# Side work of a graph-attention kernel in finer steps, and a PSUM row handed on by halves

## The chip, the cores and the metric

The kernel runs on one core of one Trainium2 chip. The metric is the device time of one execution in microseconds; the kernel before took 1645.74 us (median of three, 1645.39 to 1646.08). The core has five engines with queues of their own: TensorE (PE, matmul and transposes; PEld is its weight load), VectorE (DVE), ScalarE (ACT), GpSimd (POOL) and SyncE (SP, which issues transfers). Each works through its own instructions in order and waits where an operand or a buffer is not ready.

## The reference

Eight graphs (B = 8) of N = 2048 nodes with F = 64 features share one adjacency matrix `adj`. Four layers follow each other, each with a residual and a normalisation over the features. Layers 0 to 2 are graph attention; cut to what matters:

```python
h = x @ W                                   # layer 0 also scales x by node, and normalises h
s1, s2 = h @ a1, h @ a2                     # one score per node each
e = leaky_relu(s1[:, :, None] + s2[:, None, :], 0.2)
att = softmax(where(adj > 0, e, -big), axis=-1)
out = elu(att @ h)                          # layer 0: att @ h + h; layer 2: relu
x = layernorm(x + out)
# layer 3: softmax over neighbours of softplus features, per feature, then the same residual
```

A row without any neighbour gets the mean of `h`.

## The kernel before

A **unit** is one layer of one graph, with K = 16 steps, one for each block of 128 source nodes. There are 24 units in this order: layers 0 and 1 for graphs 0 to 3 (units 0 to 7), the same for graphs 4 to 7 (units 8 to 15), then layer 2 for all eight (units 16 to 23). Layer 3 runs beside layer 2 and after it.

In layers 0 and 1 the exponential of the leaky score is taken apart: up to a factor that softmax cancels it is `exp(s2[j]) * max(exp(0.8 s1[i]), exp(-0.8 s2[j]))`. So the kernel keeps a row `r` of exp(0.8 s1) for all 2048 nodes, spread over 128 partitions in PSUM, and one step is one VectorE instruction on 128x2048 and eight matmul records (four products of 512 columns, each in two fp32 passes):

```python
def spread(layer, b):                       # the row of the next unit, from three bf16 pieces
    sc = S[layer, b]
    sc.r = Banks.pool.tile([P, N], F32, tag="b", name=f"r_{layer}_{b}")   # one buffer of four banks
    for c in range(NCH):                    # NCH = 4
        sl = slice(c * 512, (c + 1) * 512)
        pe.matmul(sc.r[:, sl], lhsT=ones3, rhs=sc.r3[:, sl], start=True, stop=True)

def attend(u, jb, last):                    # one step; layer 2 cut
    w = work.tile([P, N], F32, tag="w", name=f"w_{u.n}_{jb}", bufs=4)
    dve.scalar_tensor_tensor(w, s.r, s.e[:, 1, jb : jb + 1], edge[:, jb, :], ALU.max, ALU.mult)
    if jb == K - 1:
        last()                              # hands over: spread() of the next unit
    for c in range(NCH):
        pe.matmul(sums[c], lhsT=s.v[:, jb, :], rhs=w[:, c * 512 : (c + 1) * 512],
                  start=(jb == 0), stop=False)
    # after the last step: the three-row product of mean and emptyT closes the sums
```

In layer 2 the step is a clamp on GpSimd, two exponentials on ScalarE into PSUM and two products of 128x1024 on VectorE.

Everything else is **side work**, written as generators. `bg.step()` is called once per step of a unit and lets each running generator go on to its next `yield`; `yield 2` lets one call pass. So a `yield` decides behind which step's instructions the rest is queued on each engine.

```python
def finish(u):                              # after a unit; cut
    for c in range(2):
        act.copy(oT[:, c], u.acc[c])        # out of PSUM
    ...
    while done < 4:
        width = Banks.width()               # PSUM tiles to use at once: 2, or 1 in layer 2
        ...                                 # per tile: two matmuls, p_o <- oT, RH
        yield 2 if pairs and width == 2 else 1      # pairs: layer 3 has begun
        ...                                 # den = 1 / p_o (DVE), o = p_o * den (ACT)
    ...                                     # residual and elu on ACT and POOL, with yields
    pool.tensor_tensor(o, o, e, ALU.add)
    e_slots.give()
    yield 1
    nm, rs = yield from stats(o, K, f"x_{u.n}")     # sums on DVE, st_x; power -1/2 on POOL
    yield 1
    for k in range(K):                      # xn <- o, normalised, 16 small ACT instructions
        ...
        if k % K2 == K2 - 1:                # K2 = 8
            yield 1

def scores(layer, b):                       # s1, s2 of the next layer of the graph; cut
    yield from transposed(xT, sums, V[layer, b].v, f"{n}v")
    p = psum(f"p_s_{n}")
    for q in range(K2):
        pe.matmul(p[:, 4 * q : 4 * q + 4], lhsT=xT[:, q], rhs=AS[layer], start=True, stop=True)
    for h in range(2):                      # the mean over the nodes, from two partial sums
        pe.matmul(p[:, 64 : 64 + F], lhsT=sums[:, h : h + 1].to_broadcast([P, P]),
                  rhs=ident2, start=(h == 0), stop=(h == 1))
    ...                                     # exponentials, row to memory, mean

def features0(b):                           # h, scores and row of layer 0; cut
    for k in range(K):
        act.activation(xs[:, k], x[:, k], AF.Identity, scale=..., bias=...)
        if k == K2 - 1:
            yield 1
    yield 1
    ...                                     # transposes, products p_h, squares, st_h
    ...                                     # row to memory (row_d)
    for k in range(K2): ...                 # y <- h, eight ACT instructions
    yield 1
    for k in range(K2, K): ...
    ...                                     # sums for the mean on POOL, p_mean
```

`prepare` fetches the next unit's row (`row`) and forms `pv` = V * exp(s2) on GpSimd once the row is there, from step 10 of the unit before; where it is not there in time the loop runs side work until it is. After units 7 and 15, `group` prepares layer 2 for four graphs at once; its core is a log-sum-exp `p_lse` of 256 small matmuls over the adjacency blocks, two row blocks at a time for the first group. Main loop, cut:

```python
for n, (layer, b) in enumerate(todo):
    now[0] = layer
    for jb in range(K):
        attend(u, jb, handover)
        if jb == K - 1:
            ...                             # finish(u), then scores(layer + 1, b), then group
        elif not done and jb >= 10 and ready(*nxt):
            prepare(*nxt); done = True
        if layer == 0 and jb == 4 and 2 <= b + 2 < B:
            bg.add(features0(b + 2))        # graphs 0 and 1: before and at unit 0
        bg.step()
    while not done:
        bg.step() ...
    handover()
```

Of the kernel before, what the change touches and what calls it, by code (L numbers as in the profile page):

```python
# [8 lines left out]
F32 = mybir.dt.float32  # L9
# [5 lines left out]
ALU = mybir.AluOpType  # L15
AX = mybir.AxisListType

P = 128
# [30 lines left out]
def gnn4_kernel(ctx: ExitStack, tc: tile.TileContext, t, out):  # L49
# [438 lines left out]
    def stats(y, n, name):  # L488

        st = small.tile([P, 2, n], F32, tag="st", name=f"st_{name}", bufs=4)  # L490
        yield from sq_slots.take()
        sq = tmp.tile([P, n, F], F32, tag="sq", name=f"sq_{name}")
        act.activation(sq, y, AF.Square)
        dve.tensor_reduce(st[:, 0], y, AX.X, ALU.add)
        yield 1
        dve.tensor_reduce(st[:, 1], sq, AX.X, ALU.add)
        sq_slots.give()
        yield from inv_std(st, n, name)
        return st[:, 0], st[:, 1]
# [88 lines left out]
    def features0(b):  # L588

        n = f"0_{b}"  # L590
        x = x_cur[b].v
        xs = early.tile([P, K, F], F32, tag="xs", name=f"xs_{b}", bufs=1)
        for k in range(K):
            act.activation(
                xs[:, k],
                x[:, k],
                AF.Identity,
                scale=nodes[:, k : k + 1],
                bias=nodes[:, K + k : K + k + 1],
            )  # L600
            if k == K2 - 1:
                yield 1
        yield 1
        yield from xT_slots.take()
        xT = tmp.tile([P, K2, P], F32, tag="xT", name=f"xT_{b}")
        sums = small.tile([P, 2], F32, tag="sums", name=f"sums_{b}", bufs=4)
        yield from transposed(xT, sums, xs, n)
        yield from h_slots.take()
        h = tmp.tile([P, K, F2], F32, tag="h", name=f"h_{b}")
        g0 = 0  # L610
        while g0 < 4:
            width = Banks.width()
            ps = []
            yield from pm_slots.take(width)
            for g in range(g0, min(g0 + width, 4)):
                p = psum(f"p_h_{b}_{g}")
                for k in range(2):
                    pe.matmul(
                        p[:, k * 2 * F2 : (k + 1) * 2 * F2],
                        lhsT=xT[:, 2 * g + k],  # L620
                        rhs=w0c.rearrange("p h f -> p (h f)"),
                        start=True,
                        stop=True,
                    )
                ps.append((g, p))
            yield 1
            for g, p in ps:
                act.copy(
                    h[:, 4 * g : 4 * g + 4, :], p[:, : 4 * F2].rearrange("p (k f) -> p k f", f=F2)
                )  # L630
            pm_slots.give(width)
            g0 += width
        xT_slots.give()
        yield from sq_slots.take()
        sq = tmp.tile([P, K, F], F32, tag="sq", name=f"sq_h_{b}")
        act.activation(sq, h[:, :, :F], AF.Square)
        yield 2
        st = small.tile([P, 2, K], F32, tag="st", name=f"st_h_{b}", bufs=4)
        dve.tensor_reduce(st[:, 1], sq, AX.X, ALU.add)
        sq_slots.give()  # L640
        yield from inv_std(st, K, f"h_{b}", centered=True)
        rs = st[:, 1]
        sc = S[0, b] = Scores()
        s = small.tile([P, 2, K], F32, tag="s0", name=f"s_{n}")
        dve.tensor_tensor(
            s, h[:, :, F:].rearrange("p k w -> p w k"), bc_k(rs, 2, K), ALU.mult
        )
        dve.tensor_tensor(s, s, bc_f(s_off, 2, K), ALU.add)
        exponentials(sc, s[:, 0], s[:, 1], s, 0, b, n)()

        yield from pm_slots.take()
        p = psum(f"p_r_{n}")
        pe.transpose(p[:K, :P], sc.e[:, 0], ident)
        yield 1
        rows_term(sc, p[:K, :P], n, 0, b)
        pm_slots.give()
        y = rows_tile(early, "y", f"y_{b}")
        for k in range(K2):
            act.activation(y.block(k), h[:, k, :F], AF.Copy, scale=rs[:, k : k + 1])
        yield 1  # L660
        for k in range(K2, K):
            act.activation(y.block(k), h[:, k, :F], AF.Copy, scale=rs[:, k : k + 1])
        y.settle()
        V[0, b] = y
        src = y.v
        for m in (8, 4, 2, 1):
            pool.tensor_tensor(h[:, :m, :F], src[:, :m], src[:, m : 2 * m], ALU.add)
            src = h[:, :, :F]
        yield 4
        yield from pm_slots.take()  # L670
        p = psum(f"p_mean_{n}")
        pe.matmul(p[:, :F], lhsT=ones, rhs=h[:, 0, :F], start=True, stop=True)
        h_slots.give()
        yield 1
        yield from mean_pieces(sc, p[:, :F], n)

    def scores(layer, b):

        n = f"{layer}_{b}"
        sc = S[layer, b] = Scores()  # L680
        yield from xT_slots.take()
        xT = tmp.tile([P, K2, P], F32, tag="xT", name=f"xTv_{n}")
        sums = small.tile([P, 2], F32, tag="sums", name=f"sumsv_{n}", bufs=4)
        yield from transposed(xT, sums, V[layer, b].v, f"{n}v")
        yield from pm_slots.take()
        p = psum(f"p_s_{n}")
        for q in range(K2):
            pe.matmul(
                p[:, 4 * q : 4 * q + 4], lhsT=xT[:, q], rhs=AS[layer], start=True, stop=True
            )  # L690
        s = p[:, : 4 * K2].rearrange("p (q r w) -> p w q r", r=2, w=2)
        for h in range(2):
            pe.matmul(
                p[:, 64 : 64 + F],
                lhsT=sums[:, h : h + 1].to_broadcast([P, P]),
                rhs=ident2,
                start=(h == 0),
                stop=(h == 1),
            )
        xT_slots.give()  # L700
        yield 1 if b == B - 1 else 2
        if layer == 2:
            g = groups2[b // NB]
            if b % NB == 0:
                g.s = small.tile([P, 2, NB, K], F32, tag="s", name=f"s_{n}", bufs=1)
            act.copy(g.s[:, :, b % NB].rearrange("p w (q r) -> p w q r", r=2), s)
            bg.add(mean_pieces(sc, p[:, 64 : 64 + F], n), begun=True)
        else:
            s1 = small.tile([P, 2, K], F32, tag="s0", name=f"s_{n}")
            act.copy(s1.rearrange("p w (q r) -> p w q r", r=2), s)  # L710
            top = exponentials(sc, s1[:, 0], s1[:, 1], s1, layer, b, n)
            bg.add(mean_pieces(sc, p[:, 64 : 64 + F], n), begun=True)
            yield from pm_slots.take()
            p = psum(f"p_r_{n}")
            pe.transpose(p[:K, :P], sc.e[:, 0], ident)
            yield 1
            top()
            rows_term(sc, p[:K, :P], n, layer, b)
            pm_slots.give()
# [24 lines left out]
    def spread(layer, b):  # L744

        sc = S[layer, b]
        sc.r = Banks.pool.tile([P, N], F32, tag="b", name=f"r_{layer}_{b}")
        for c in range(NCH):
            sl = slice(c * 512, (c + 1) * 512)
            pe.matmul(sc.r[:, sl], lhsT=ones3, rhs=sc.r3[:, sl], start=True, stop=True)  # L750
# [6 lines left out]
    def group(gi):  # L757
# [61 lines left out]
        yield 1  # L819

        am = small.tile([P, NB, K], F32, tag="am", name=f"am_{nm}", bufs=1)
        slots = pl_slots if Banks.shared else pm_slots
        yield from slots.take()
        Banks.busy += 1
# [74 lines left out]
    def attend(u, jb, last):  # L899

        s = u.s
        if u.layer < 2:
            w = work.tile([P, N], F32, tag="w", name=f"w_{u.n}_{jb}", bufs=4)
            dve.scalar_tensor_tensor(
                w, s.r, s.e[:, 1, jb : jb + 1], edge[:, jb, :], ALU.max, ALU.mult
            )
        else:
            w = ahead[u.b, jb]
            if jb + 2 < K:
# [27 lines left out]
    def finish(u):  # L937
# [16 lines left out]
        while done < 4:  # L954
# [16 lines left out]
            done += width  # L971
            if done >= 4:
                oT_slots.give()
            yield 2 if pairs and width == 2 else 1
            for c, s0, p in ps:
                p4 = p[:, : 4 * F1].rearrange("p (s h f) -> p s h f", s=2, h=2)
                den = small.tile([P, 2, 2], F32, tag="den", name=f"den_{u.n}_{c}_{s0}")
# [22 lines left out]
        else:  # L1000
# [15 lines left out]
            yield 1  # L1016
            pool.tensor_tensor(o, o, e, ALU.add)
            e_slots.give()
            yield 1
        nm, rs = yield from stats(o, K, f"x_{u.n}")  # L1020
        xn = Rows(x_cur[b].t, layer < 2)
        if layer == 2:
# [3 lines left out]
        else:  # L1026
            yield 1
            for k in range(K):
                act.activation(
                    xn.block(k), o[:, k], AF.Identity, scale=rs[:, k : k + 1], bias=nm[:, k : k + 1]  # L1030
                )
                if k % K2 == K2 - 1:
                    yield 1
            xn.settle()
        o_slots.give()
# [7 lines left out]

    pairs = []

    now = [0]

    def l3_features(b):

# [199 lines left out]
    def flags():  # L1249
# [12 lines left out]
        dve.tensor_tensor(beyond[0:1, :], beyond[0:1, :], top[0:1, 1:2], ALU.max)  # L1262
        dve.tensor_scalar(flag, beyond[0:1, :], 0.0, None, ALU.is_gt)

    for n, (layer, b) in enumerate(todo):
        if (layer, b) == (2, 1):
            early_.close()
# [2 lines left out]
        if (layer, b) == (2, 5):  # L1270
            bg.add(flags())
        u = unit(layer, b)
        now[0] = layer
        nxt = todo[n + 1] if n + 1 < len(todo) else None
        done = nxt is None

# [6 lines left out]
        def handover():  # L1283
# [3 lines left out]
            if in_psum(*nxt):  # L1287
                if n == 0:
                    Banks.use("psR", 1)
                spread(*nxt)  # L1290
            elif nxt == (2, 0):
                Banks.use("psE", 2)
# [4 lines left out]
        for jb in range(K):  # L1297
# [22 lines left out]
                load_x(b + 4)  # L1320
            if n == 0 and jb == 3:
                bg.add(constants())
            if layer == 0 and jb == 4 and 2 <= b + 2 < B:
                bg.add(features0(b + 2))
            bg.step()
        while not done:
            bg.step()
# [515 lines left out]
```

## Time and profile before

| | busy us | share of the span of 1643.8 us |
|---|---|---|
| PE, matmuls | 1349.0 | 82% |
| PE, weight loads (beside matmuls) | 667.2 | 41% |
| DVE | 1301.1 | 79% |
| ACT | 802.8 | 49% |
| POOL | 823.7 | 50% |

The parts of the run, cut where the closing matmuls of units 0, 15 and 23 end:

| part | from, to (us) | PE busy | DVE busy | POOL busy |
|---|---|---|---|---|
| start and unit 0 | 0 to 105.7 | 61.0 | 71.8 | 26.4 |
| units 1 to 15, layers 0 and 1 | 105.7 to 839.2 | 622.4 | 631.1 | 254.8 |
| units 16 to 23, layer 2 beside layer 3 | 839.2 to 1396.5 | 469.9 | 465.8 | 435.2 |
| rest of layer 3 | 1396.5 to 1643.8 | 195.7 | 132.5 | 107.3 |

How to read the lines that follow in the prediction. Instructions are named by engine, operation and tiles, output before the arrow and inputs after it: `w<-r,se,edge` is the product of one step. All carry L78, the line of a helper that records every instruction, so tiles are what tells them apart. A timeline line gives the start in us, the length, the instruction, its shape and how many were merged; in brackets stands how long the engine had been idle before it and what ended the wait. A line of waits gives who waited for whom, us in total, times, and the longest. PEclk is the clock granted to TensorE, in tenths of full speed.

### The profile page before, as it was taken

The page shows a single profiled execution, that of the slowest core. Times are in us where ns is not written, and L with a number is a line of the kernel's source. Part 1 is how long each engine was busy: PE and PEld are TensorE (multiplying, and loading weights), DVE is VectorE, ACT ScalarE, POOL GpSimd, SP SyncE. Part 2 cuts the span into 40 slices and gives each one's busy share as a digit, 9 for nine tenths or more (in the row PEclk, how much of TensorE's full clock was granted, in tenths as well). Part 3 has the DMA queues.
Part 4 walks back from the last instruction along what each step waited for, and adds up shares of the span by engine and source line. Part 5 has one row for each costly group of instructions (what it writes and reads, how often), then busy time and mean ns, then how long its engine had stood idle before and what let it go on. Part 6 is the DMA issues. An engine that isn't in the chain of part 4 may idle for free.

```text
span 1643.8 us, 20952 instructions
## 1 busy us (share of the span) xinstructions
PE 1349.0 (82%) x8162; PEld 667.2 (41%) x8162; DVE 1301.1 (79%) x1334; ACT 802.8 (49%) x1635; POOL 823.7 (50%) x726
## 2 busy tenths in 40 slices
PE   3687879888888898888887676699896999587996
PEld 2222323333333343233322231165452545476885
DVE  4888877899887989898888878969897977738444
ACT  5234664443265443442378857676656664242111
POOL 2145353422222454321257748877789877546332
PEclk9999988899998999999999878899998999888998
DMA  8800000000000000000000000000010000000000
GB/s 329 215 5 1 1 2 1 1 2 1 1 1 2 1 2 2 2 1 26 26 1 26 26 1 27 0 26 8 30 33 7 4 4 11 10 4 14 11 14 19
DMA packets 42190, 36.86 MB, mean 22 GB/s; under 512 B 37509, under 2 KB 37813, under 8 KB 39906
## 3 DMA queue, kind: packets, MB, share of 16 engines
q1 hardware_dynamic: 41538, 34.26, 6.8%
q8 instruction: 66, 1.08, 0.3%
q10 hardware_dynamic: 544, 1.17, 0.2%
q14 instruction: 42, 0.34, 0.1%
HBM read 30.94 MB, written 4.45 MB: 22 GB/s over the span
## 4 chain that ended last, share of the span: by engine, by line
PE 31%; DVE 17%; ACT 7%; POOL 4%; issue 3%; POOLq 0%; DVEq 0%; ACTq 0%
PE p_l L78 18%; PE acc L78 11%; DVE w L78 10%; ACT e L78 3%; DVE o L78 2%; DVE st_x L78 2%; DVE x L78 1%; POOL v L78 1%; PE p_o L78 1%; ACT x L78 1%; POOL vf L78 1%; DVE f L78 1%; PE p_s L78 1%; POOL w L78 1%; POOL o L78 1%
## 5 line engine op out<-in xcount | busy, mean ns | idle before, releaser
L78 PE MATMUL acc<-w,pv 128*64 128x512 f32 x2048 | 525.4, 642 | 117.0 <-DVE w L78 95.1
L78 DVE SCALAR_TENSOR_TENSOR w<-r,se,edge 128x2048 f32<-128x2048 f32 x240 | 551.9, 2340 | 27.1 <-PE r L78 26.3
L78 PEld LDWEIGHTS <-edge 128*128 128x128 fp8e4 x3842 | 321.2, 99 | 153.1 <-issue 94.3
L78 PE MATMUL p_l<-v,edge 128*128 128x256 bf16 x3072 | 351.1, 275 | 37.4 <-ACT nd L78 13.1
L78 PE MATMUL acc<-w,x 128*64 128x512 f32 x1024 | 281.8, 667 | 87.4 <-DVE w L78 79.9
L78 ACT ACTIVATE e<-w,s_g 128x1024 f32<-128x1024 f32 x256 | 277.6, 1113 | 148.1 <-DVE w L78 103.7
L78 DVE TENSOR_TENSOR w<-e,edge 128x1024 f32<-128x1024 f32 x256 | 300.3, 1214 | 56.3 <-ACT e L78 54.2
L78 PEld LDWEIGHTS acc<-w,pv 128*64 128x64 f32 x2048 | 134.9, 143 | 401.6 <-issue 199.5
L78 POOL TENSOR_SCALAR w<-row,hi_g,lo_g 128x2048 f32<-128x2048 f32 x128 | 270.5, 2118 | 37.6 <-PE acc L78 33.4
L78 PEld LDWEIGHTS acc<-w,x 128*64 128x64 f32 x1024 | 64.0, 146 | 231.9 <-DVE w L78 154.7
L78 POOL TENSOR_TENSOR eh<-eh,x 128x1024 f32<-128x1024 f32 (+2 forms) x24 | 36.5, 1533 | 153.2 <-ACT eh L78 153.2
L78 ACT ACTIVATE nd<-p_l,empty 128x256 f32<-128x256 f32 x64 | 30.1, 470 | 158.8 <-PE p_l L78 158.8
L78 ACT ACTIVATE x<-o,st_x 128x64 f32<-128x64 f32 x256 | 87.4, 432 | 26.9 <-DVE st_x L78 26.9
L78 ACT COPY oT<-acc 128x512 f32<-128x512 f32 x48 | 25.7, 587 | 122.6 <-PE acc L78 122.5
L78 ACT ACTIVATE o<-p_o,den 128x64 f32<-128x64 f32 x256 | 56.2, 323 | 48.5 <-DVE den L78 48.4
L78 DVE RECIPROCAL den<-p_o 128x4 f32<-128x4 f32 x96 | 16.9, 179 | 73.5 <-PE p_o L78 59.5
L78 POOL TENSOR_TENSOR st_h<-isw_h,mhalf 128x16 f32<-128x16 f32 x8 | 23.6, 2956 | 99.2 <-DVE isw_h L78 94.9
L78 PEld LDWEIGHTS p_o<-rh,oT 128*128 128x128 f32 x384 | 51.2, 200 | 53.5 <-issue 32.0
L78 POOL TENSOR_TENSOR st_x<-isw_x,mhalf 128x16 f32<-128x16 f32 x24 | 70.5, 2936 | 2.0
L78 PE MATMUL p_o<-rh,oT 128*128 128x130 f32 x384 | 64.0, 302 | 7.9 <-ACT o L78 5.6
L78 POOL TENSOR_SCALAR isw<-isw 128x4 f32<-128x4 f32 x32 | 8.5, 265 | 122.6 <-DVE isw L78 122.5
L78 DVE TENSOR_REDUCE st<-sq 128x4 f32<-128x256 f32 x32 | 13.2, 414 | 70.4 <-ACT sq L78 70.3
(233 smaller groups left out, 1511.5 us busy)
## 6 DMA issues: line engine op xcount, KB each, us to landing
raw<-in_adjT_dram SPq DMA_DIRECT2D x8, 1024.0 KB
raw<-in_adjT_dram SPq DMA_DIRECT2D x16, 512.0 KB
row<-rows_d_g SPq DMA_DIRECT2D x8, 1024.0 KB
x<-in_x_dram SPq DMA_DIRECT2D x8, 512.0 KB
out_dram<-o SPq DMA_DIRECT2D x64, 64.0 KB
row<-row_d ACTq DMA_DIRECT2D x1, 1024.0 KB
row_d<-rT SPq DMA_DIRECT2D x15, 12.0 KB
row<-row_d SPq DMA_DIRECT2D x15, 12.0 KB
```

What stands on the lines that cost most here:

```text
L78: ins = f(*args, **kwargs)
```

## The change

The change reorders the side work of layers 0 and 1 and takes one matmul out of each mean.

- The row `r` has one PSUM tile for all units instead of a new allocation of the same buffer for each, and the first and last product of a unit are split in two halves, so that the row can pass to the next unit half by half.
- The reciprocals of a finish come two steps behind their matmuls wherever two PSUM tiles are used; the statistics come one step later, and in layers 0 and 1 their second part again one later; the normalised rows are written in four steps instead of two.
- Scores take two steps for their eight products in layers 0 and 1, and GpSimd adds the two partial sums, so that the mean needs one product instead of two.
- Features of layer 0 for graphs 4 to 7 go in finer steps, and most start beside other units: graphs 2 to 5 began beside units 0 to 3 and 6, 7 beside units 8, 9, at step 4. Now 2 and 3 begin at step 1 of units 0 and 1, and 4, 5, 6, 7 at step 4 of units 4, 5, 6 and 8.
- The first log-sum-exp waits until unit 12.

```diff
     def stats(y, n, name):
         dve.tensor_reduce(st[:, 0], y, AX.X, ALU.add)
-        yield 1
+        yield 2 if now[0] < 2 else 1
         dve.tensor_reduce(st[:, 1], sq, AX.X, ALU.add)
...
     def features0(b):
+        step = K2 if b < NB else 4          # NB = 4
...
-            if k == K2 - 1:
+            if k % step == step - 1:
                 yield 1
-        yield 1
...
         dve.tensor_reduce(st[:, 1], sq, AX.X, ALU.add)
         sq_slots.give()
+        if b >= NB:
+            yield 1
...
-        for k in range(K2):
-            act.activation(y.block(k), ...)
-        yield 1
-        for k in range(K2, K):
+        for k in range(K):
             act.activation(y.block(k), ...)
+            if k % step == step - 1 and k < K - 1:
+                yield 1
...
     def scores(layer, b):
+        pool.tensor_tensor(sums[:, 0:1], sums[:, 0:1], sums[:, 1:2], ALU.add)
         for q in range(K2):
             pe.matmul(p[:, 4 * q : 4 * q + 4], ...)
+            if q == K2 // 2 - 1 and now[0] < 2:
+                yield 1
-        for h in range(2):
-            pe.matmul(..., lhsT=sums[:, h : h + 1].to_broadcast([P, P]), ...)
+        pe.matmul(..., lhsT=sums[:, 0:1].to_broadcast([P, P]), ..., start=True, stop=True)
...
     def spread(layer, b):
-        sc.r = Banks.pool.tile([P, N], F32, tag="b", name=f"r_{layer}_{b}")
+        sc.r = Banks.r                      # allocated once, at the first handover
...
     def group(gi):
         am = small.tile(...)
+        while now[1] < 3 * NB:
+            yield 1
         ...                                 # p_lse
...
     def attend(u, jb, last):                # layers 0 and 1
-            dve.scalar_tensor_tensor(w, s.r, s.e[:, 1, jb : jb + 1], edge[:, jb, :], ...)
+            parts = 2 if jb in (0, K - 1) and in_psum(u.layer, u.b) else 1
+            for c in range(parts):
+                sl = slice(c * (N // parts), (c + 1) * (N // parts))
+                dve.scalar_tensor_tensor(w[:, sl], s.r[:, sl], ..., edge[:, jb, sl], ...)
...
     def finish(u):
-            yield 2 if pairs and width == 2 else 1
+            yield 2 if width == 2 else 1
...
             pool.tensor_tensor(o, o, e, ALU.add)
             e_slots.give()
-            yield 1
+            yield 2
...
-                if k % K2 == K2 - 1:
+                if k % 4 == 3:
                     yield 1
...
+    begin = {0: 2, 1: 3, 4: 4, 5: 5, 6: 6, 8: 7}
-        now[0] = layer
+        now[:] = layer, n
...
-            if layer == 0 and jb == 4 and 2 <= b + 2 < B:
-                bg.add(features0(b + 2))
+            if jb == (1 if n < 2 else 4) and n in begin:
+                bg.add(features0(begin[n]))
```

More of the change, by code (lines that the diff above doesn't have):

```diff
@@ L657, in features0 @@
         y = rows_tile(early, "y", f"y_{b}")
-        for k in range(K2):
+        for k in range(K):
             act.activation(y.block(k), h[:, k, :F], AF.Copy, scale=rs[:, k : k + 1])
-        yield 1
-        for k in range(K2, K):
-            act.activation(y.block(k), h[:, k, :F], AF.Copy, scale=rs[:, k : k + 1])
+            if k % step == step - 1 and k < K - 1:
+                yield 1
         y.settle()
@@ L690, in scores @@
             )
+            if q == K2 // 2 - 1 and now[0] < 2:
+                yield 1
         s = p[:, : 4 * K2].rearrange("p (q r w) -> p w q r", r=2, w=2)
-        for h in range(2):
[L693 to L699, printed above, removed]
+        pe.matmul(
+            p[:, 64 : 64 + F],
+            lhsT=sums[:, 0:1].to_broadcast([P, P]),
+            rhs=ident2,
+            start=True,
+            stop=True,
+        )
         xT_slots.give()
@@ L903, in attend @@
             w = work.tile([P, N], F32, tag="w", name=f"w_{u.n}_{jb}", bufs=4)
-            dve.scalar_tensor_tensor(
-                w, s.r, s.e[:, 1, jb : jb + 1], edge[:, jb, :], ALU.max, ALU.mult
-            )
+            parts = 2 if jb in (0, K - 1) and in_psum(u.layer, u.b) else 1
+            for c in range(parts):
+                sl = slice(c * (N // parts), (c + 1) * (N // parts))
+                dve.scalar_tensor_tensor(
+                    w[:, sl],
+                    s.r[:, sl],
+                    s.e[:, 1, jb : jb + 1],
+                    edge[:, jb, sl],
+                    ALU.max,
+                    ALU.mult,
+                )
         else:
@@ L1044, in gnn4_kernel @@
     pairs = []
-    now = [0]
+    now = [0, 0]
     def l3_features(b):
@@ L1289, in handover @@
                     Banks.use("psR", 1)
+                    Banks.r = Banks.pool.tile([P, N], F32, tag="b", name="r")
                 spread(*nxt)
```

## The prediction

> **What bounds the kernel now.** I read the page's busy times first, then its forty slices, then busy time by stretch, then the waits of VectorE and TensorE, and last the timelines around one change of unit.
>
> ```profile
> PE 1349.0 (82%) x8162; PEld 667.2 (41%) x8162; DVE 1301.1 (79%) x1334; ACT 802.8 (49%) x1635; POOL 823.7 (50%) x726
> ...
> DVE  4888877899887989898888878969897977738444
> ...
> PEclk9999988899998999999999878899998999888998
> ```
>
> No engine is full. Two are near it, PE and DVE, and they take turns. Everything the change touches with weight lies in the units of layers 0 and 1. In the trace their matmuls that close a unit (the three-row product with `emptyT`) end at 105.7 us for unit 0 and at 839.2 us for unit 15, so fifteen units take 733.5 us, 48.9 us each. I asked for busy time in those fifteen stretches, cut at these ends; three lines of the answer (columns: length, then PE, weight loads, DVE, ACT, POOL busy, granted clock, DMA):
>
> ```profile
> 208.70:269.70 61.00, 49.88 (x216) 20.94 (x212) 47.11 (x36) 35.79 (x117) 26.10 (x33) 0.80 0.01 2
> ...
> 369.40:412.70 43.30, 37.35 (x184) 13.50 (x180) 39.99 (x28) 16.47 (x48) 9.96 (x8) 1.00 0.01 1
> ...
> sum 733.50, PE 622.41 PEld 238.92 DVE 631.06 ACT 326.38 POOL 254.82; mean PE 41.49 PEld 15.93 DVE 42.07 ACT 21.76 POOL 16.99
> ```
>
> The best unit (unit 6, with no features of layer 0 beside it) takes 43.3 us, the worst (unit 3, with two sets of features beside it) 61.0 us. DVE is busy 42.07 us of a mean 48.9: it is the tighter engine, and 102 us of the stage is DVE idle. Sixteen products `w` at 2340 ns make 37.4 us of its 42. What it waits for in this stage, and one line of PE's own waits (us in total, times, longest):
>
> ```profile
> DVE den L78 <- PE p_o L78: 35.5, 40, 4.7
> DVE w L78 <- PE r L78: 26.3, 14, 5.8
> DVE st_x L78 <- POOL o L78: 10.7, 6, 3.6
> DVE den L78 <- issue: 7.6, 5, 3.6
> DVE den L78 <- ACT o L78: 5.7, 3, 2.0
> ```
>
> ```profile
> PE acc L78 <- DVE w L78: 76.1, 90, 5.2
> ```
>
> So two waits carry the idle time, both at the change of unit: the reciprocals `den` wait for the matmuls `p_o` of the finished unit (35.5 + 7.6 + 5.7 = 48.8 us), and the first product of a unit waits for its row `r` in PSUM (26.3 us). One change of unit, on DVE and then on PE:
>
> ```profile
> 314.00 2.35 DVE L78 SCALAR_TENSOR_TENSOR w<-r,se,edge 128x2048 f32<-128x2048 f32 x1
> 319.07 4.61 DVE L78 SCALAR_TENSOR_TENSOR w<-r,se,edge 128x2048 f32<-128x2048 f32 x2 [2.73 <-PE r L78]
> ...
> 329.16 0.18 DVE L78 RECIPROCAL den<-p_o 128x4 f32<-128x4 f32 x1 [3.26 <-PE p_o L78]
> ```
>
> ```profile
> 302.18 3.58 PE L78 MATMUL p_s<-as,xTv 128*128 128x4 f32 x16
> ...
> 312.70 5.37 PE L78 MATMUL acc<-w,pv 128*64 128x512 f32 x24
> 318.00 1.03 PE L78 MATMUL r<-row,ones 3*128 3x512 bf16 x4
> ```
>
> The last product ends at 316.35 us, but `r` is written only from 318.00: PE stands in its backlog, which began with the clump of sixteen score matmuls (3.58 us) at 302. Then DVE, with two products of lead, meets the reciprocals and stands 3.26 us although the next product could run.
>
> [...] after an idle stretch of 4.31 us eight `acc` records take 3.68 us, against 1.94 elsewhere, and unit 3 had a mean granted clock of 0.80.
>
> ```profile
> 244.35 3.68 PE L78 MATMUL acc<-w,pv 128*64 128x512 f32 x8 [4.31 <-DVE w L78]
> 247.97 3.58 PE L78 MATMUL p_s<-as,xTv 128*128 128x4 f32 x16
> ```
>
> [...] the trace before shows `r` only handed on whole. [...] PE's busy 622 us of this stage hides 76.1 us of waits for DVE and stretches at half clock.
>
> **The change, part by part.**
>
> 1. Row by halves. A single `r` tile stays allocated for all fifteen units, and the first and last product of each are split in two. While the second half of the last product runs (about 1.2 us), PE can write the first two chunks (half of the 1.03 us above, so 0.5 us) and the next unit's first half can follow without a gap. Some ten of the 14 waits are the plain 1.1 us of this kind (558.66 us, for instance); three are large (5.8, 4.2, 2.7) and come from PE's backlog or a late row. Halves cost: in layer 2 a product of 128x1024 takes 1214 ns, twice that is 2428 against 2340, so 88 ns for each of 2 x 15 split products: 2.6 us of DVE.
>
> 2. The late row. The 5.8 us wait came before unit 3: its row was sent to memory at 207.0 us and fetched at 209.6, with the unit due at 208.7. Its features begin now at step 1 of unit 1 instead of step 4: three steps of some 2.6 us, 8 us earlier. That wait, and the 4.90 us that PE then lost on `pv`, should go. Parts 1 and 2 together: 26.3 to about 6, so 20 us.
>
> 3. Reciprocals one step later. With two PSUM tiles in hand the finish now yields twice, so one more `w` (2.34 us) stands ahead of the `den` pair. The 48 waits for `den` average 1.0 us and none is longer than 4.7; only what exceeds 2.3 should stay. I take 48.8 to 16: 33 us.
>
> 4. Statistics later (yield 2 ahead of and within them), normalised rows in four steps instead of two. The wait of `st_x` for POOL's sum (10.7 us) should halve: 5 us.
>
> 5. Scores in two steps of four products, and one product less per mean. PE saves one product of two fp32 passes, half of the four records that take 0.57 us at full clock and 1.03 at half: 0.3 to 0.5 us, fourteen times, 4 to 7 us of PE. POOL gets 14 additions of 128x1; the nearest rows are its 128x16 ones at 207 to 265 ns, so 0.25 us each, 4 us on an engine that is busy for 255 of 733 us. PE's work falls to some 617 us. None of this is counted alone; it is what lets part 1 work.
>
> 6. Features moved: before, 2 to 5 beside units 0 to 3 and 6, 7 beside units 8, 9; after, 2, 3 beside units 0, 1, then 4, 5, 6 beside units 4, 5, 6 and 7 beside unit 8. The first log-sum-exp goes from units 9 and 10 (54.5 and 49.3 us) to unit 12, which had 39.3 us of PE in 48.3; eight bursts of 0.9 us make 7.2 us of PE. This adds and removes nothing. Units 3, 9 and 10 should fall to about 46 to 48, units 4 to 7 stay near 47, unit 12 stays near 48.
>
> Sum: 20 + 33 + 5 - 2.6 = 55 us of DVE idle time less. I choose to keep four fifths of it, 45 us, since at 685 us for the stage PE (617) would be 90% busy and DVE (634) 93%, and two engines so full will wait for each other somewhere new. The start up to 105.7 us, layer 2 (839.2 to 1396.5) and the tail keep their programs but for one product per mean and some steps in the last finish of layer 1, whose log-sum-exp has slack: its rows leave at 987.8 us, and the first unit that needs one begins at 1093.2 us, the end of unit 19. I put them at zero. 1645.7 - 45 = 1601 us.
>
> **Rivals.** *PE becomes the bound.* The side work now runs on past the change of unit and meets the next unit's `p_o`, so `den` waits for a fuller PE. For it: unit 10 was already PE's (48.0 busy of 49.3). Against: the mean PE busy is 41.5 of 48.9, some of it at half clock. The gain is then 15 to 20 us: about 1627. *The work only moves.* What leaves units 3, 9 and 10 comes back in 4 to 6 and 12, and a longer finish delays rows. Against: rows of layer 1 have three units of slack. Then 1635 to 1645. *The clock helps too.* A mean clock of 0.94 over 733.5 us means some 88 us at half speed, 44 us of PE's work lost. If fewer DVE stalls leave fewer idle windows, half of that comes back beside the DVE waits, and the stage loses 65 us: about 1580. For it: two of the half-clock stretches follow DVE stalls (244 and 151 us). Against: other stretches follow no long stall.
>
> **Range and chances.** 1601 us, with 1578 to 1632 eight times in ten: the low end is the clock rival, the high end the PE rival with a little given back. Faster by over 2% means below 1612.8, a gain of 33 us, three fifths of the counted 55: 0.66. Within 2%: 0.29. Slower: 0.05, for a new wait that I have not seen.
>
> **What would show it.** Right: DVE's wait for `r` below 8 us in this stage, its waits for `den` below 20, unit 3 below 50 us, DVE busy above 90% of the stage, layer 2 within 5 us of 557. Half tiles of about 1.2 us at both ends of a unit, and `r` written in two pairs with a product between. Wrong: `w` waiting for `r` as before (the tile is not handed on by halves after all), `den` waits as large though a product later, PE idle gone but units still at 48 us (PE is the bound), or units 4 to 6 above 52 us.

## The result and the profile after

The changed kernel takes 1584.59 us (median of four, 1580.78 to 1589.69), the kernel before 1645.57 in the same comparison: a ratio of 0.9632, 95% interval 0.9605 to 0.966. The gain is 61 us; 45 were predicted.

The page of the changed kernel, the lines that answer to those of before:

```profile
PE 1332.2 (84%) x8130; PEld 657.5 (42%) x8130; DVE 1289.7 (81%) x1366; ACT 800.3 (51%) x1635; POOL 830.2 (52%) x740
...
DVE  4798989988999999899879898787978796837444
...
PEclk9998989999999999899998878999999999798998
```

The digits of DVE in the first half of the span mostly went up (their sum from 158 to 167); in the second half they did not (140 and 139). Cut at the closing matmuls again, the parts are: start and unit 0 105.0 us (before 105.7), units 1 to 15 667.8 (733.5), layer 2 561.0 (557.3), the rest 248.8 (247.3). So the whole gain, 66 us, is in the units of layers 0 and 1; 5 us go back later. The stretch of unit 6 and the sum over units 1 to 15 (columns as before: length, PE, weight loads, DVE, ACT, POOL busy, clock, DMA):

```profile
340.50:389.40 48.90, 40.68 (x197) 15.74 (x197) 41.78 (x37) 29.72 (x97) 19.33 (x26) 0.97 0.01 2
...
sum 667.80, PE 601.67 PEld 231.70 DVE 619.49 ACT 317.77 POOL 254.87; mean PE 40.11 PEld 15.45 DVE 41.30 ACT 21.18 POOL 16.99
```

Unit 3 fell from 61.0 to 50.8 us, unit 6 rose from 43.3 to 48.9, since features now run beside it. DVE is busy 93% of the stage (619.5 of 667.8), before 86%. Its longest waits in this stage:

```profile
DVE w L78 <- PE r L78: 19.7, 11, 6.2
DVE st_x L78 <- POOL o L78: 14.5, 5, 5.2
DVE den L78 <- PE p_o L78: 5.9, 8, 1.9
```

The waits for `den` are nearly gone (48.8 to 6.8 us, with 0.9 in a smaller line); PE's waits for DVE's products fell from 76.1 to 40.0 us. Those for `r` fell little, those for POOL's sum rose. Read alone, this list says that the reciprocals brought 42 of the 66 us. The experiments say otherwise.

**What became of the halves.** DVE and then PE at the handover to unit 11:

```profile
557.09 2.47 DVE L78 SCALAR_TENSOR_TENSOR w<-r,se,edge 128x1024 f32<-128x1024 f32 x2
560.67 2.48 DVE L78 SCALAR_TENSOR_TENSOR w<-r,se,edge 128x1024 f32<-128x1024 f32 x2 [1.11 <-PE r L78]
```

```profile
559.61 1.02 PE L78 MATMUL r<-row,ones 3*128 3x512 bf16 x4 [0.88 <-DVE w L78]
```

Both halves of the last product end at 559.56 us. Only then do the four chunks run, in one piece to 560.63, and only then begins the first half of the next product. It is so at all fourteen handovers where the last product read the PSUM row. In the program only the first of the four chunk matmuls carries a wait for DVE, for both halves, and only the first half of the next product a wait for PE, for all four chunks. Nothing is handed on by halves.

### The profile page after: what moved, and what is told of

Its sections match the earlier page's. It is cut to its first block, busy times and chain, and to the rows that moved or that the text cites. A ratio compares the mean times of both kernels' runs of the same rounds, so it can differ in the third digit from the quotient of the medians.

```text
span 1582.6 us, 20958 instructions
## 1 busy us (share of the span) xinstructions
PE 1332.2 (84%) x8130; PEld 657.5 (42%) x8130; DVE 1289.7 (81%) x1366; ACT 800.3 (51%) x1635; POOL 830.2 (52%) x740
## 4 chain that ended last, share of the span: by engine, by line
PE 30%; DVE 22%; ACT 7%; POOL 5%; issue 4%; POOLq 0%; DVEq 0%; ACTq 0%
PE p_l L78 18%; DVE w L78 14%; PE acc L78 10%; ACT e L78 4%; DVE st_x L78 2%; DVE o L78 2%; POOL w L78 1%; POOL v L78 1%; POOL vf L78 1%; ACT x L78 1%; PE p_o L78 1%; DVE x L78 1%; ACT L78 1%; DVE f L78 1%; DVE nd L78 1%
## 5 line engine op out<-in xcount | busy, mean ns | idle before, releaser
L78 DVE SCALAR_TENSOR_TENSOR w<-r,se,edge 128x2048 f32<-128x2048 f32 (+1 forms) x270 | 555.5, 2102 | 22.6 <-PE r L78 19.7
L78 PE MATMUL acc<-w,pv 128*64 128x512 f32 x2048 | 507.3, 628 | 66.0 <-DVE w L78 60.8
L78 PE MATMUL acc<-w,x 128*64 128x512 f32 x1024 | 286.5, 671 | 84.9 <-DVE w L78 78.3
L78 ACT ACTIVATE o<-p_o,den 128x64 f32<-128x64 f32 x256 | 56.0, 325 | 48.8 <-DVE den L78 48.8
L78 POOL CAST rT<-rT 16x128 bf16<-16x128 f32 x45 | 15.0, 333 | 99.9 <-ACT rT L78 96.8
L78 POOL TENSOR_SCALAR isw_x<-isw_x 128x16 f32<-128x16 f32 x24 | 6.5, 269 | 98.5 <-DVE isw_x L78 98.0
```

The lines of the kernel that those rows point to most:

```text
L78: ins = f(*args, **kwargs)
```

## The experiments

Two theories stood at first. D: the later reciprocals carry the gain, as the waits suggest. R or F: moving the features and the log-sum-exp away from crowded units carries it. A third, P, came to stand for the finer steps of scores, statistics and rows. Parts were undone one at a time in the changed kernel, or added to the kernel before, and timed beside the kernel before. The single row tile and the finer steps within the features were not tried alone.

| kernel | median us | ratio to before, 95% interval | units 1 to 15, us |
|---|---|---|---|
| changed kernel | 1584.6 | 0.9632 (0.9605 to 0.966) | 668 |
| without halves | 1581.9 | 0.9605 (0.9582 to 0.9629) | 661 |
| old scores | 1595.3 | 0.969 (0.9664 to 0.9717) | 676 |
| without later reciprocals | 1605.7 | 0.9751 (0.9735 to 0.9767) | 690 |
| old features | 1617.7 | 0.9819 (0.9796 to 0.9842) | 702 |
| old statistics | 1628.1 | 0.9889 (0.9859 to 0.9919) | 707 |
| before + later log-sum-exp | 1657.7 | 1.0088 (1.0059 to 1.0117) | 740 |
| the same + reciprocals | 1639.5 | 0.9963 (0.9949 to 0.9976) | 720 |
| the same + statistics | 1617.1 | 0.9817 (0.9796 to 0.9838) | 700 |
| the same + both | 1609.9 | 0.9773 (0.9752 to 0.9794) | 694 |

The last column is read from the one execution with a trace. It took about the median but for the old features, where it took 1624.5 us. The start, up to the end of unit 0, takes 105 to 106 us in the first two traces (before and changed) and 107 to 110 in all others, the unchanged start of the kernel before with the later log-sum-exp among them: 2 to 4 us of a difference between a later run and the changed kernel need not come from the edit.

### The log-sum-exp alone

```diff
+        while now[1] < 3 * NB:          # kernel before; now[1] is the unit
+            yield 1
```

> The kernel before with one part of the change: the first log-sum-exp waits for unit 12. Theory D (the later reciprocals carry the gain): 1640 to 1650 us, no difference beyond noise, since it removes no wait of DVE for den or r. Theory R (relief of the crowded units 3, 9 and 10 carries it): units 9 and 10 (103.8 us together before) fall by 8 us or more and come back by less at unit 12, 1632 to 1640 us.

Measured: 1657.7 us, 0.9% slower than before. Unit 9 stays at 54.5 us, units 10 and 12 rise by 3 to 4 us each and unit 16 by 11. It relieves nothing alone, and R fails here. Unit 9 had nothing to lose: in the trace before, all 256 products of the first log-sum-exp stand beside unit 10. Unit 10 did lose 8 us of PE work (48.0 to 40.0) and still rose, so PE was not what held it. In unit 16 DVE's waits for the exponentials of ACT grew from 5.6 to 17.6 us, but layer 2 as a whole is only 3 us longer; why is open. Undoing this part alone in the changed kernel was not tried.

### The reciprocals on top of it

```diff
-            yield 2 if pairs and width == 2 else 1
+            yield 2 if width == 2 else 1
```

> The same, and the reciprocals of a finish come two steps behind their matmuls where two PSUM tiles are used. Theory D: DVE's waits for den in units 1 to 15 fall from 48.8 us below 12, and the time with them: 1605 to 1618 us. Theory R: den is only where a crowded PE shows, so the wait moves to the next product or to r and the time falls by under 10 us against the run before: above 1625 us.

Measured: 1639.5 us, 18 us less than without. Neither expectation holds: the time stayed above theory D's 1618, and the gain above theory R's 10. DVE's waits in units 1 to 15, first with the log-sum-exp alone, then with the reciprocals too:

```profile
DVE den L78 <- PE p_o L78: 39.4, 41, 4.6
DVE w L78 <- PE r L78: 24.8, 14, 6.2
DVE st_x L78 <- POOL o L78: 17.9, 7, 5.8
```

```profile
DVE w L78 <- PE r L78: 34.8, 13, 13.5
DVE st_x L78 <- POOL o L78: 29.8, 10, 8.8
DVE den L78 <- PE p_o L78: 12.1, 9, 6.4
```

The `den` waits went nearly as theory D said (with the smaller lines for `den`, from 50 to 14 us). But of some 36 us, 22 came back in two other places: everything behind `den` in the chain of a finish is a step later now, so DVE meets the sum `o` of POOL before it is there (12 us more), and rows come later (10 us more; the waits ahead of units 3 and 4 are 10.1 and 13.5 us, with the log-sum-exp alone 6.2 and 4.2).

### Statistics, alone and with the reciprocals

```diff
         dve.tensor_reduce(st[:, 0], y, AX.X, ALU.add)
-        yield 1
+        yield 2 if now[0] < 2 else 1
...
             pool.tensor_tensor(o, o, e, ALU.add)
             e_slots.give()
-            yield 1
+            yield 2
...
-                if k % K2 == K2 - 1:
+                if k % 4 == 3:
```

> The kernel before with the later log-sum-exp and the statistics and normalised rows in the later, finer steps, without the later reciprocals. Waits for POOL's sum were 17.9 us without these steps. Theory A (the parts add): the steps are worth 10 to 15 us alone, 1643 to 1648 us. Theory C (the later reciprocals need them, and they need the reciprocals): they alone give under 8 us, 1650 to 1658 us.

> The same with both, the later reciprocals and the later statistics; features, scores and halves stay as before. With the reciprocals alone den waits fell to 12 us but st_x waits rose to 30. Theory C: with both, den and st_x stand below 15 us each, and the time falls by 25 us or more against 1639.5: 1600 to 1615 us. Theory A: 1622 to 1630 us.

Measured: 1617.1 us with the statistics alone, 40.6 us less; 1609.9 with both, 47.8 less. Against 18.2 for the reciprocals alone the two overlap (18.2 + 40.6 = 58.8), so they neither add nor need each other, and both theories had the statistics far too small. (1609.9 lies in theory C's range for both parts, but not by its reason: the statistics do not need the reciprocals.) All this is counted from the later log-sum-exp, which costs 10 us itself; against the kernel before, it and the statistics bring 30 us together. The waits with the statistics alone, then with both:

```profile
DVE w L78 <- PE r L78: 25.4, 11, 7.7
DVE den L78 <- PE p_o L78: 20.6, 39, 1.6
DVE st_x L78 <- POOL o L78: 7.5, 3, 4.0
```

```profile
DVE w L78 <- PE r L78: 42.6, 12, 10.3
DVE st_x L78 <- POOL o L78: 9.8, 5, 4.0
DVE den L78 <- PE p_o L78: 3.6, 5, 1.4
```

The later sums take 10 us of `st_x` waits away, as meant, but also half of the `den` waits, which they do not touch. The side work of a finish falls beside other steps now, and PE's granted clock in the stage is higher (0.96 against 0.94); which of the two shortens `den` is not settled. With both parts `den` and `st_x` are small and `r` stands alone at 42.6 us.

### The features

```diff
-            if jb == (1 if n < 2 else 4) and n in begin:      # changed kernel
-                bg.add(features0(begin[n]))
+            if layer == 0 and jb == 4 and 2 <= b + 2 < B:
+                bg.add(features0(b + 2))
```

> The changed kernel with the features of layer 0 begun where they were before (graphs 2 to 5 at step 4 of units 0 to 3, 6 and 7 at step 4 of units 8 and 9), all else as changed. The reciprocals account for some 21 us of the gain of 61; theory F (the move of the features carries most of the rest): 1605 to 1620 us, with units 1 to 3 above 50 us and rows that come late again. Theory P (finer steps of scores, statistics and rows carry the rest): 1585 to 1595 us.

Measured: 1617.7 us, 33 us more, as theory F said; but of units 1 to 3 only unit 3 is clearly above 50 us (45.5, 50.0 and 52.6), and the loss against the changed kernel lies in units 2, 4, 5 and 9. The first line of its waits:

```profile
DVE w L78 <- PE r L78: 45.3, 12, 10.0
```

Three of these waits, 10.0, 9.6 and 9.7 us, stand ahead of the first products of units 3, 4 and 5. The kernel with both parts above, whose features begin as before, has the same three (9.3, 10.2 and 10.3 us). So that is what the move is for: with features of graphs 2 to 5 all beside units 0 to 3, the longer chains bring three rows about 10 us late each; with only 2 and 3 there, and begun earlier, the waits for `r` are 19.7 us in all.

### The scores, the statistics and the reciprocals undone

```diff
-        pool.tensor_tensor(sums[:, 0:1], sums[:, 0:1], sums[:, 1:2], ALU.add)
-            if q == K2 // 2 - 1 and now[0] < 2:
-                yield 1
-        pe.matmul(..., lhsT=sums[:, 0:1].to_broadcast([P, P]), ...)
+        for h in range(2):
+            pe.matmul(..., lhsT=sums[:, h : h + 1].to_broadcast([P, P]), ...)
```

> The changed kernel with scores in one step of eight products and two products for the mean. Theory P: the clump of some 3 us stands before the handover again, waits for r rise by 10 us, 1595 to 1605 us. Theory F: PE has room, only the 4 to 7 us of PE work come back and half of that shows, 1585 to 1590 us.

> The changed kernel with statistics and normalised rows in the steps of before. Theory P: 1592 to 1600 us, since DVE meets sums that are not there yet. Theory F: DVE's wait for POOL's sum is 14.5 us in the changed kernel, no less than the 10.7 before, so these steps buy little: 1582 to 1588 us.

> The changed kernel with the reciprocals one step behind again. Theory D: den waits of 35 to 45 us come back, 1615 to 1630 us. Theory R: most of the gain stays, 1590 to 1600 us.

Old scores: 1595.3 us, 11 us more. That is theory P's number, but not by its reason: the waits for `r` did not rise (17.9 us). DVE's idle time is as in the changed kernel (48 us), and its busy time 8 us longer (627.3 against 619.5), the whole of what the stage gained in length. Of the 8 us, 4 lie in the `mean` instructions and 2 in one `s` of 2.27 us, whose like take 0.19. Its line, and POOL's beside it:

```profile
420.70 2.27 DVE L78 TENSOR_TENSOR s<-s,s_off 128x32 f32<-128x32 f32 x1
```

```profile
420.58 2.34 POOL L78 TENSOR_TENSOR o<-o,eh 128x1024 f32<-128x1024 f32 x1
```

The two end within 0.05 us of each other, and so does every other small DVE instruction that took long in this stage, within 0.1 us of one on POOL (more on this at the end). So most of these 11 us are, by my estimate from the 6 of 8 us above, small instructions of DVE that took long beside POOL's, and not the clump. Why the old scores bring more of that is open; they also differ in two things at once, the clump and the second product of the mean.

Old statistics: 1628.1 us, 43 us more, the largest of all parts, of the kind that theory P said but 28 us beyond its range:

```profile
DVE st_x L78 <- POOL o L78: 38.0, 12, 6.8
```

Without the later reciprocals: 1605.7 us, 21 us more, between the two theories (theory D needs 30 or more, theory R 15 or less). Its longest wait in total is `den` again (26.3 us in 44 times). The stretch of its units 1 to 15:

```profile
107.80:798.00 690.20, 595.62 (x3064) 225.12 (x3064) 633.25 (x517) 319.48 (x1002) 255.56 (x263) 0.99 0.01 4
```

The granted clock is 0.99 here against 0.95 in the changed kernel, and the stage is 22 us longer all the same, with 26 us more of PE's waits for DVE's products (66.2 us). Here the higher clock did not go with the shorter stage.

### The halves

```diff
-            parts = 2 if jb in (0, K - 1) and in_psum(u.layer, u.b) else 1
+            parts = 1
```

> The changed kernel with whole products at both ends of a unit; the single row tile stays. In the trace of the changed kernel PE begins a row only after both halves of the last product, and the first half of the next waits for all four chunks. So theory W (the halves hand nothing on): 30 second instructions less, at 0.12 us each 3.6 us of DVE, 1578 to 1583 us with waits for r as they were (20 us). Theory H (the halves help): waits for r rise by 10 us or more, 1592 to 1600 us.

Measured: 1581.9 us. The waits for `r` are what they were with halves:

```profile
DVE w L78 <- PE r L78: 20.5, 11, 6.5
```

So theory W holds: the halves hand nothing on. Their cost is 30 pairs at 2.47 us against single products of 2.34, 3.9 us by the traces. The medians differ by 2.7 us, with intervals that overlap.

### Versions of my own

```diff
# spaced: without halves, and
-    begin = {0: 2, 1: 3, 4: 4, 5: 5, 6: 6, 8: 7}
+    begin = {0: 2, 1: 3, 3: 4, 5: 5, 7: 6, 9: 7}
# own_a: without halves, graph 3 earlier, statistics a step later; own_b: the same on top of spaced
-    begin = {0: 2, 1: 3, ...}
+    begin = {0: 2, ...}
+            if n == 0 and jb == 13:
+                bg.add(features0(3))
             pool.tensor_tensor(o, o, e, ALU.add)
-            yield 2
+            yield 3
```

> A version of my own: the changed kernel without the halves, and with the features of graphs 4 to 7 begun beside every second unit (3, 5, 7, 9) instead of 4, 5, 6, 8. Units 5 and 6, 49 us each in the changed kernel with st_x waiting for POOL 9.5 us in them, carry two sets of features in part at once. Theory F: one set at a time brings them to 43 to 45 us, 1570 to 1577 us. If crowding no longer costs anything: 1580 to 1584 us as without the halves alone.

> A version of my own: the changed kernel without halves, the features of graph 3 begun at step 13 of unit 0 instead of step 1 of unit 1, and the statistics of layers 0 and 1 one step later still. In the changed kernel unit 3 waits 6.2 us for its row and three st_x waits make 13.5 us. If both go and nothing comes in their place: 1581.9 - 20 = 1562 us; if the later side work meets the next unit's: 1575 to 1585 us.

> The same with the features of graphs 4 to 7 begun beside units 3, 5, 7 and 9. Spread like that the st_x waits of units 5 and 6 were 4.9 us instead of 9.6 but came back in other units; with the statistics a step later they go everywhere: 1560 to 1568 us, a little below the version before it or equal to it.

Measured: spaced 1583.4 us, own_a 1580.8 (ratio 0.9608, 0.9588 to 0.9628), own_b 1577.1 (0.9571, 0.9552 to 0.9591). Spacing did bring units 5 and 6 down, from 48.7 and 48.9 us without the halves to 45.9 and 42.9, but units 10 and 11 rose by 9 together, and the time is the one expected if crowding costs nothing. own_a, too, lies in the range given for no gain. The early features removed the wait of unit 3 (50.9 us without the halves, 43.5 in own_a, 42.3 in own_b). The trace of own_b is of the slowest of its five executions, 1583.1 us; the others took 1574.3 to 1578.9. Its waits in units 1 to 15 are

```profile
DVE w L78 <- PE r L78: 22.1, 10, 4.6
DVE den L78 <- PE p_o L78: 12.4, 6, 6.1
DVE st_x L78 <- POOL o L78: 4.1, 2, 2.1
```

against 20.5, 0.9 and 14.6 without the halves: the waits of `st_x` went and those of `den` came back. own_b is the fastest kernel here, 7.5 us below the changed one by the medians, with intervals just apart; the hoped 1560 to 1568 us were not reached.

## Why the prediction was right, and where it was not

The time lay in the range, 16 us below the middle, and the mechanism was right: DVE idle between products at the change of unit, ended by later side work. DVE's idle time in the stage fell by 54 us (102 to 48), the 55 of the sum before the discount. That these two agree is luck, since the terms of the sum are far off, and some 9 us of waits went that no term held (those for `lc_g` and `mean`, 4.9 and 4.6 us before). Of the signs named, three did not come: `r` below 8 us, unit 3 below 50 (50.8), and `r` written in two pairs.

- *Part 1, the row by halves* failed. The waits for `r` fell to 19.7 us, not to 6, and the split costs 3.9 us, not 2.6. That PE can write one half while DVE still reads the other was my assumption. No run shows such a handover, since the program waits for the row whole: one such row begins at 559.61 us, 0.05 us after both halves of the product have ended. The diff said what was meant, and I did not ask which waits would come of it.
- *Part 2, the late row* was half right. The row of unit 3 was fetched at 194.6 us instead of 209.6, ahead of the close of unit 2 at 199.1, but DVE still waited 6.2 us: in PE's order the row stands behind a transpose `p_r` that waits for ACT.

```profile
201.58 0.28 PE L78 MATMUL p_r<-ident,se 128*16 128x128 f32 x1 [2.44 <-ACT se L78]
201.79 1.11 PE L78 MATMUL r<-row,ones 3*128 3x512 bf16 x4
```

- *Part 3, the reciprocals*: the waits fell to 6.8 us, further than the 16 predicted. But the wait taken away was not time gained: the part is worth 18 us on top of the later log-sum-exp and 21 in the whole, not 33.
- *Part 4, the statistics*, is the mis-sized term: 5 us predicted, 41 us on top of the later log-sum-exp and 43 in the whole. I sized it by the one wait in the list that it touches (10.7 us). That wait does not even fall in the changed kernel (14.5 us); without the steps it would be 38.
- *Part 5, the scores*, counted for nothing alone, is worth 11 us, but not as the help to part 1 that it was meant to be: most of it is DVE busy time. The four records of a mean take 0.64 us at a granted clock of 1.00 (192.63 us in the trace before) and 1.09 at 0.50 (251.40 us), a little more than the 0.57 and 1.03 I read.
- *Part 6, the features*, "adds and removes nothing": it is worth 33 us once the chains are longer. The log-sum-exp stood beside unit 10 only, not beside 9 and 10 as I read it. Units 9 and 10 fell to 40.2 and 47.6 us; units 4 to 6 stayed below the 52 that would have told against it.
- *The discount* of a fifth for two engines so full was not needed: PE is busy 90% and DVE 93%, as estimated (for a stage of 685 us; 733.5 less 45 is 688.5, which changes nothing), and the gain of the stage is larger than the sum. Part of it is 11.6 us less of DVE busy time, which no term held.
- *The rivals*: PE did not become the bound (its waits for DVE are still 40.0 us). The clock rival had the size, 65 us. The clock did rise, from a mean of 0.94 to 0.95: in the stage before it was granted at 0.50 for 88.7 us in 16 stretches, in the changed stage for 61.4 us in 11, and at 1.00 otherwise. But the run at 0.99 is slower; no run changes the clock alone, so its share in the shorter waits stays open. Layer 2 and the tail lost 5 us, which I had at zero.

The four parts undone one by one cost 11, 21, 33 and 43 us, 108 together, for a gain of 61, so they are not independent. In part one cures the waits that others cause, as with `st_x` and `r` above. In part it is DVE's busy time, which is 8 to 14 us longer in each of the four traces than in the changed kernel's (619.5 us), 38 together.

## What to carry to other kernels

Moving one instruction later moved its whole chain here: with the reciprocals a step later the `den` waits fell by some 36 us, and 22 came back behind them. So measure such a move with and without the steps behind it, and look at the next wait of the chain, here from `den` to `st_x` to the row. Compare busy times as well as waits. Size such a part by what comes back when it is undone in the final kernel as well as by the wait it removes in the first. Where a buffer is to pass in pieces, look in the trace for the consumer between the pieces before you count on it.

## What the runs showed of the hardware

Some small DVE instructions took far longer than others of their kind and ended together with a large one of POOL. In the kernel before, `isw_h`, 128x16, takes 174 ns in the median, but once 2.19 us. The line on DVE, and POOL's beside it:

```profile
238.63 2.19 DVE L78 TENSOR_SCALAR isw_h<-st_h 128x16 f32<-128x16 f32 x1
```

```profile
238.43 2.36 POOL L78 TENSOR_TENSOR o<-o,eh 128x1024 f32<-128x1024 f32 x1 [2.92 <-ACT o L78]
```

POOL began 0.20 us earlier, and the two end within 0.03 us of each other. What made `isw_h` take that long no run shows. In the changed kernel the six `isw_h` take 160 to 175 ns, and the 41 `mean` instructions of DVE a mean of 319 ns against 427.

It is so throughout the stage. I estimate the time lost by what each DVE instruction other than the products took above the median of its kind over all traces, where that is over 0.15 us. In the kernel before these are 11 instructions and 10.5 us, in the changed kernel one and 1.9 us; so by this estimate most of the 11.6 us less of DVE busy time came from here. With one of the four parts undone they are 8 to 13 instructions and 9 to 12 us, with parts added to the kernel before 11 to 14 instructions and 12 to 15 us, in the four versions of the changed kernel without halves 3 to 5 instructions and 4 to 8 us. Every one of them ends within 0.1 us of a POOL instruction beside it; in the kernel before and the changed one it is 0.03 to 0.08 us later than POOL's. No run moves such an instruction alone, and whether the changed kernel has few of them by chance or by its finer steps is open.
